# A graph layer on one core: the second pair's norm one call later, x + h on GpSimd, and the first matrix quarter loaded ahead of the second block of x

## The chip, the cores and the metric

One core of one Trainium2 chip. The metric is the device time of one launch in microseconds (us). The kernel before takes 1369.55 us, the median of three runs (1368.07 to 1371.08).

The core's engines are named as the profile names them: PE (TensorE, matrix products and transposes, results in PSUM), PEld (its weight load), DVE (VectorE), ACT (ScalarE), POOL (GpSimd) and SP (SyncE, which here only issues transfers). SPq and ACTq are the queues on which SP and ACT issue DMA transfers. Each engine works through its own instructions strictly in the order of the program and waits on semaphores for the others.

## The reference

A relational graph layer with a gate, over N = 1250 nodes of D = 1024 features and 20000 edges of 8 types, all in float32:

```python
h = relu(layernorm(x))
u = h @ root + bias
for r in range(8):
    mask = (edge_type == r)
    sums = segment_sum(h[src] * mask[:, None], dst, N)
    cnt = segment_sum(mask, dst, N)
    u = u + (sums / max(cnt, 1)[:, None]) @ weight[r]
z = concat([u, h], axis=1) @ w_gate + b_gate
out = x + tanh(u) * z + h * (1 - z)
```

The output can be written as (x + h) + z * (tanh(u) - h). The kernel stores x + h early, in the DRAM tensor `xh_dram`, and fetches it again in its last stage.

## The kernel before

**Matrix passes.** There are eleven matrices of 1024 x 1024: eight weights, root, and the two halves of w_gate. Pass s multiplies h by matrix s (s = 0 to 9); the last pass, with u, is written out separately. h is held in transposed form, five pairs of 128-row blocks: pair i is the blocks i and i + 5, in the buffer `h_op[i]`. A product of one pair with one matrix is `product()`: a Strassen form with seven products of quarters of 512 x 512 instead of eight. Seven operands come from each side: A11, A12, A21, A22 are the transposed quarters of h, and S1 to S4 are sums of them made by `left()` on DVE (L275). On the matrix side b11, b12, b21 and b22 are loaded quarters, and t1 to t4 are differences made by `make_t1()` to `make_t4()` on DVE (L167, L171, L175, L179). b12 is loaded into t3's buffer by `load_next()`.

After each quarter product PE goes on with the next; its PSUM bank is taken over by ACT (copies L330, L337, L341, L316, L359) or DVE (L309, L317, L325). PE accumulates in two banks, b and c, so it must wait for the copy out of b before it may add the next but one product into it: before S2 for L330, before S3 for L341.

**The order of the work.** The schedule is written by hand: whatever is called first stands first on its engine's queue. `product()` calls `between(j)` after each of its quarter products (j = 0 to 6). In pass 0, `between` takes one step of the generator `index()`, which runs two generators side by side: `norms()` (the layer norm, transposes and stores of the pairs 1 to 4) and `columns()` (the edge tables). A `yield` in `norms()` thus means "go on after the next quarter product". Pass 0, pair 0 has its own order: after A11 comes `second_block()`, which transposes the second block and makes the operands, then A12, S1, S2, S4, S3, A22.

**One pair's norm.** `both(a, b)` gives the order for the two blocks of a pair: statistics on DVE (L579, L583), the square root on ACT (L584), reciprocal and the negated scaled mean on DVE (L588, L589, both on 128 x 1), then h = relu(scale * x + less) on ACT (L605). `store()` writes h to `h_dram` from SP's queue; `factored()` transposes it on PE and evicts it, A11 or A21 on ACT (L266), A12 or A22 on DVE (L264). `with_x()` adds x + h on DVE (L615, 128 x 1024) and issues its store on SP's queue (L616). The sums of pair 2 write into h's own place or into the buffer of x; x of its first block lies in the S1 and S2 places of `h_op[2]`, so `left(h_op[2])` must come after that sum. The h of pairs 0, 2, 3 and one block of pair 4 share the scratch in `h_op[4]`. The buffers named `xt` are three, used in turn: a later load of x waits for the x + h store of the block that had the buffer.

**The start.** At the top, SP's queue carries the first half of each of the two x blocks of pair 0, then b11 (`load_first()`), b21, b12, b22, the x of pair 1 and of pair 2, then the edge lists. ACT's queue carries the second halves of the two x blocks. Block 0 is normed in halves on DVE (`centre(2)`, L598), transposed, and its relu is in the eviction (L262, L266); block 5 is normed with two relus on ACT (`relu(2)`), and `second_block()` transposes it. The relu of block 0's own h, L686, comes after that.

GpSimd makes the identity and a few fills at the start, the two iotas of `columns()`, and two fills of the last block's padding; from 124 us on it issues the scatters and gathers of the edges.

Of the kernel before, what the change touches and what calls it, by code (L numbers as in the profile page):

```python
# [19 lines left out]
def tile_rgcn_highway(  # L20
# [31 lines left out]
    nc = tc.nc  # L52
# [37 lines left out]
    def nrows(d):  # L90
        return min(P, N - d * P)
# [4 lines left out]
    def nedges(c):  # L96
        return P if c < NCH - 1 else EL
# [83 lines left out]
    class Second:  # L181
# [22 lines left out]
        def left(self):  # L204
            nc.vector.tensor_add(self.s1, self.a21, self.a22)
            nc.vector.tensor_sub(self.s2, self.s1, self.a11)
            nc.vector.tensor_sub(self.s3, self.a11, self.a21)
            nc.vector.tensor_sub(self.s4, self.a12, self.s2)
# [43 lines left out]
    def transposed(aop, part, of, n, relu=False):  # L252


        for half, to in enumerate(((A11, A12), (A21, A22))[part]):
            p = bank().rearrange("p (k f) -> p k f", k=KQ)
            for i in range(KQ):
                k = KQ * half + i
                nc.tensor.transpose(p[:, i, :n], of[:n, k * P:(k + 1) * P], ident[:n, :n])  # L259
            to_n, p_n = aop[:, to, :, :n], p[:, :, :n]  # L260
            if half and relu:
                nc.vector.tensor_scalar_max(to_n, p_n, 0.0)  # L262
            elif half:
                nc.vector.tensor_copy(to_n, p_n)  # L264
            else:
                nc.scalar.activation(to_n, p_n, AF.Relu if relu else AF.Copy)  # L266
            if n < P:
                nc.gpsimd.memset(aop[:, to, :, n:], 0.0)
# [103 lines left out]
    fac = []  # L372
# [173 lines left out]
    with ExitStack() as early:  # L546
# [6 lines left out]
        def load_x(i, part, t=None, pieces=1):  # L553
            d = i + part * NP
            n = nrows(d)
            if t is None:
                t = xpool.tile([P, D], F32, name="xt")
            for j in range(pieces):
                at = slice(j * D // pieces, (j + 1) * D // pieces)
                (nc.scalar if j else nc.sync).dma_start(t[:n, at], x[d * P:d * P + n, at])  # L560
            return t

        def scratch(i, part):

            return h_op[i][:, 2 * part:2 * part + 2].rearrange("p a k f -> p (a k f)")

        class Normed:
# [44 lines left out]
            def with_x(self, to=None):  # L612
                n = self.n
                to = self.xt if to is None else to
                nc.vector.tensor_add(to[:n], self.xt[:n], self.ht[:n])  # L615
                nc.sync.dma_start(xh_dram[self.d * P:self.d * P + n, :], to[:n])  # L616

        def both(a, b):

            a.stats(0)  # L620
            a.stats(1)
            a.spread()
            b.stats(0)
            a.scale()
            a.relu()
            b.stats(1)
            b.spread()
            b.scale()
            b.relu()

        def factored(i, blocks):
            for part in range(2):
                transposed(h_op[i], part, blocks[part].ht, blocks[part].n)


        warm = xpool.tile([P, 1], F32, name="warm")
        x0 = [load_x(0, part, pieces=2) for part in range(2)]
        nc.scalar.activation(warm, eps, AF.Sqrt)
        fac[0].load_first()
        fac[0].load_b21()  # L640
        fac[0].load_next()
        fac[0].load_b22()
# [21 lines left out]
        b0 = [Normed(part * NP, x0[part], scratch(NP - 1, part)) for part in range(2)]  # L664
# [285 lines left out]
                    yield  # L950

        def norms():
            yield
            yield
            both(*b1)
            fac[0].make_t4()
            for b in b1:
                b.store()
            yield
            yield  # L960
            yield
            factored(1, b1)
            left(h_op[1])
            yield
            for b in b0:
                b.with_x()
            x3 = [load_x(3, part) for part in range(2)]
            b2 = [Normed(2 + part * NP, x2[part], scratch(NP - 1, part)) for part in range(2)]
            both(*b2)
            yield  # L970
            for b in b2:
                b.store()
            yield
            for b in b1:
                b.with_x()
            yield
            factored(2, b2)
            b2[0].with_x(b2[0].ht)
            b2[1].with_x()
            left(h_op[2])  # L980
            x4 = [load_x(4, 0)]
            yield
            yield
            b3 = [Normed(3 + part * NP, x3[part], scratch(NP - 1, part)) for part in range(2)]
            both(*b3)
            yield
            for b in b3:
                b.store()
            yield
            factored(3, b3)  # L990
            left(h_op[3])
            yield
            for b in b3:
                b.with_x()
            x4.append(load_x(4, 1))
            yield
            for part in range(2):
                ht = xpool.tile([P, D], F32, name="xt") if part else scratch(NP - 1, 1)
                b = Normed(4 + part * NP, x4[part], ht)
                b.stats(0)  # L1000
                b.stats(1)
                b.spread()
                b.scale()
                b.relu()
                b.store()
                yield
                transposed(h_op[4], part, b.ht, b.n)
                b.with_x()
                yield
            left(h_op[4])  # L1010
            first_part.close()

        def index():
            for _ in zip_longest(norms(), columns()):
                yield
            with tc.tile_pool(name="ix", bufs=2) as ix:
                yield from slots(ix)
            yield from order()
# [17 lines left out]
    with ExitStack() as edges_part:  # L1036
# [167 lines left out]
        with tc.If(passes > 0):  # L1204
# [30 lines left out]
            with tc.For_i(0, passes, 1):  # L1235
# [9 lines left out]
                for c in range(NCH):  # L1245
                    n = nedges(c)
# [117 lines left out]
        for i in range(NP):  # L1364
# [55 lines left out]
            else:  # L1420
                product(h_op[i % 2], fac[NM - 1], t, between=beside_last, last=finish_last,
                        pieces=2, second=lambda: None,
# [24 lines left out]
```

## Time and profile before

The profile is of one execution, which took 1366.53 us by the clock of the runs; its span, from first to last instruction, is 1364.7 us.

| | |
|---|---|
| median of the runs | 1369.55 us |
| profiled execution | 1366.53 us |
| its span | 1364.7 us |
| PE busy | 1349.9 us, 99% |
| DVE busy | 932.9 us, 68% |
| POOL busy | 638.8 us, 47% |
| ACT busy | 365.7 us, 27% |
| PE busy in 0 to 104 us | 95.31 us |
| PE busy in 104 to 1364.7 us | 1254.59 of 1260.7 us |
| POOL busy in 0 to 104 us | 2.08 us |
| granted PE clock | full throughout |
| L615, one x + h on DVE | 1.22 us |
| L275, one sum of operands | 0.69 us |
| one quarter product on PE (eight instructions) | about 3.45 us |

The busy shares are averages over the whole kernel. What can change the time is where PE stands still, and that is read from the waits. A line of the timeline gives start, length, engine, line of the code, operation, output and inputs, shape, how many instructions it merges, and in brackets how long its engine had stood idle before it and what released it.

### The profile page before, as it was taken

What the parts mean: (1) busy time and instruction counts of PE and PEld (TensorE: products, weight loads), DVE (VectorE), ACT (ScalarE), POOL (GpSimd) and SP (SyncE); (2) the same over time, 40 slices, a digit from 0 to 9 for tenths busy, and PEclk for the clock granted to TensorE, in tenths of its full rate; (3) what the DMA queues carried; (4) which work ended last, traced back from release to release, by engine and by line L of the source; (5) the groups of instructions that cost most, each with busy time, mean ns of one, the idle gap of its engine ahead of it and who ended that gap; (6) DMA issues with size and microseconds to landing.
All of it is one profiled execution on the core that took longest, in us unless ns stands there. A gap on an engine that the chain in (4) does not pass through costs nothing.

```text
span 1364.7 us, 12816 instructions
## 1 busy us (share of the span) xinstructions
PE 1349.9 (99%) x3810; PEld 659.9 (48%) x3810; DVE 932.9 (68%) x1849; ACT 365.7 (27%) x792; POOL 638.8 (47%) x571
## 2 busy tenths in 40 slices
PE   8999999999999999999999999999999999999998
PEld 4444455455445544544554454455445445544443
DVE  6855887887885946567565756765664586567985
ACT  3235566566631111111111111111111111121220
POOL 0002655665561464557774435465443344435641
PEclk9999999999999999999999999999999999999999
DMA  8654565855663175379788627787965664586861
GB/s 312 253 196 131 121 139 134 191 115 114 158 167 93 61 206 137 116 250 254 218 282 315 213 81 287 264 303 258 347 217 201 217 239 149 194 284 219 294 205 58
DMA packets 110202, 272.77 MB, mean 200 GB/s; under 512 B 25956, under 2 KB 27986, under 8 KB 110000
## 3 DMA queue, kind: packets, MB, share of 16 engines
q0 software_dynamic: 48912, 128.60, 29.5%
q1 hardware_dynamic: 45088, 111.34, 26.3%
q10 hardware_dynamic: 16128, 31.98, 7.9%
q8 instruction: 30, 0.49, 0.2%
q14 instruction: 44, 0.36, 0.1%
HBM read 214.20 MB, written 80.65 MB: 216 GB/s over the span
## 4 chain that ended last, share of the span: by engine, by line
PE 91%; issue 4%; DVE 2%; POOL 1%; DMA 1%; ACT 0%; SPq 0%; POOLq 0%; DVEq 0%; ACTq 0%
PE ps L292 82%; PE ps L212 8%; PE ps L259 1%; PE ps_n L802 1%; DMA w<-in_L_gnn_weight_dram 1%; POOL out_dram L496 1%; DVE h_op L275 0%; PE ps_q L853 0%; POOL got L490 0%; DMA xt<-in_x_dram 0%; DVE st L579 0%; DMA xh_dram<-xt 0%; DVE h_op L615 0%; DVE w L171 0%; DVE h_op L264 0%
## 5 line engine op out<-in xcount | busy, mean ns | idle before, releaser
L292 PE MATMUL ps<-w,h_op 128*128 128x512 f32 x2800 | 1224.5, 593 | 6.2 <-ACT row L341 2.6
L292 PEld LDWEIGHTS ps<-w,h_op 128*128 128x128 f32 x2800 | 526.6, 190 | 620.2 <-issue 601.5
L1061 POOL DMA_INDIRECT got<-y,idx x202 | 256.0, 1267 | 265.7 <-DVE u L1069 197.2
L1069 DVE SCALAR_TENSOR_TENSOR u<-got,w_of,u 128x1024 f32<-128x1024 f32 (+1 forms) x192 | 246.0, 1283 | 127.6 <-DMA got<-y,idx 125.1
L881 POOL DMA_INDIRECT table<-row_col,at_i x157 | 180.2, 1148 | 154.1 <-DVE at_i L877 73.3
L317 DVE TENSOR_TENSOR row<-row,part 128x512 f32<-128x512 f32 x55 | 38.0, 690 | 109.6 <-ACT part L316 109.6
L359 ACT COPY row<-ps 128x512 f32<-128x512 f32 x50 | 29.3, 585 | 239.0 <-PE ps L292 234.1
L316 ACT COPY part<-ps 128x512 f32<-128x512 f32 x55 | 32.2, 585 | 179.8 <-PE ps L292 176.6
L309 DVE TENSOR_TENSOR row<-row,ps 128x512 f32<-128x512 f32 x54 | 36.9, 684 | 57.3 <-PE ps L292 53.3
L330 ACT COPY row<-ps 128x512 f32<-128x512 f32 x55 | 32.2, 586 | 163.2 <-PE ps L292 163.2
L337 ACT COPY row<-ps 128x512 f32<-128x512 f32 x55 | 32.2, 586 | 147.9 <-PE ps L292 144.3
L212 PE MATMUL ps<-w,w 128*128 128x256 f32 x288 | 71.3, 380 | 0.0
L341 ACT COPY row<-ps 128x512 f32<-128x512 f32 x55 | 32.2, 586 | 139.3 <-PE ps L292 139.3
L212 PEld LDWEIGHTS ps<-w,w 128*128 128x128 f32 x288 | 54.4, 190 | 20.9 <-issue 15.3
L807 DVE TENSOR_TENSOR seen<-seen,ps_n 128x110 f32<-128x110 f32 x157 | 42.1, 268 | 25.1 <-PE ps_n L802 20.8
L867 DVE SCALAR_TENSOR_TENSOR junk<-k_bc,key_col,before 128x128 f32<-128x128 int32 x157 | 54.9, 350 | 4.2
L527 POOL DMA_INDIRECT node_dram<-ids,pos_i x30 | 37.4, 1247 | 43.2 <-issue 42.9
L212 PE MATMUL ps<-w,h_op 128*128 128x256 f32 x216 | 56.0, 382 | 0.0
L935 DVE SCALAR_TENSOR_TENSOR junk<-v_bc,val,one 128x1280 bf16<-128x1280 f32 x30 | 46.6, 1554 | 9.5 <-DMA v_bc<-val_dram 8.7
L212 PEld LDWEIGHTS ps<-w,h_op 128*128 128x128 f32 x216 | 40.5, 190 | 25.3 <-issue 22.2
L784 ACT ACTIVATE is_lo<-io,less_lo 128x128 bf16<-128x128 f32 x157 | 50.1, 391 | 4.8 <-DMA xh_dram<-xt 4.8
L490 POOL DMA_INDIRECT u<-u_dram,node x20 | 22.9, 1145 | 51.3 <-DMA last_dram<-u 34.9
(187 smaller groups left out, 957.8 us busy)
## 6 DMA issues: line engine op xcount, KB each, us to landing
y<-row SPq DMA_DIRECT2D x72, 512.0 KB, 5.6
w<-in_L_gnn_weight_dram ACTq DMA_DIRECT2D x21, 1024.0 KB, 10.1
w<-in_L_gnn_weight_dram SPq DMA_DIRECT2D x11, 1024.0 KB, 13.3
k_bc<-keys_dram SPq DMA_DIRECT2D x39, 256.0 KB, 4.2
l_bc<-los_dram SPq DMA_DIRECT2D x39, 256.0 KB, 8.4
w<-in_L_gnn_w_gate_dram ACTq DMA_DIRECT2D x6, 1024.0 KB
h_dram<-h_op SPq DMA_DIRECT2D x9, 512.0 KB, 2.9
hr_dram<-row SPq DMA_DIRECT2D x9, 512.0 KB, 6.7
```

What stands on the lines that cost most here:

```text
L212: nc.tensor.matmul(p, a[:, k, :], b[:, k, :], start=(fresh and k == 0), stop=(k == 1), skip_group_check=True)
L292: nc.tensor.matmul(b[:, at], aop[:, i, k, :], w.of[i][:, k, at], start=(fresh and k == 0), stop=(k == KQ - 1), skip_group_check=True)
L309: nc.vector.tensor_add(c12, c12, c)
L317: nc.vector.tensor_add(c22, c22, d)
L527: ins = nc.gpsimd.indirect_dma_start(out=node_dram[g][:, :], out_offset=bass.IndirectOffsetOnAxis(ap=pos_i[:, g, d:d + 1], axis=0), in_=id ...
L784: nc.scalar.activation(is_lo[:, i, :], io, AF.Abs, bias=less_lo[:, c0 + i:c0 + i + 1])
L807: nc.vector.tensor_add(seen[j][:, i, :], was, p[:, i, :])
L867: nc.vector.scalar_tensor_tensor(junk, o["k_bc"][:, i, :], key_col[:, c:c + 1], before, op0=OP.is_equal, op1=OP.mult, accum_out=rank[:, c: ...
L881: ins = nc.gpsimd.indirect_dma_start(out=table[:, :], out_offset=bass.IndirectOffsetOnAxis(ap=at_i[:n, i:i + 1], axis=0), in_=row_col[:n, ...
L935: nc.vector.scalar_tensor_tensor(junk, v_bc[:, g, :], val[:, c:c + 1], one.to_broadcast([P, KEYS]), op0=OP.is_gt, op1=OP.mult, accum_out=p ...
L1061: nc.gpsimd.indirect_dma_start(out=t[:n], out_offset=None, in_=y[g][:, :], in_offset=bass.IndirectOffsetOnAxis(ap=at[:n, d, k:k + 1], axis=0),
L1069: nc.vector.scalar_tensor_tensor(u[:n], t[:n], w, u[:n], op0=OP.mult, op1=OP.add)
```

## The change

Three edits, all in pass 0. In `with_x()` the addition is issued on GpSimd instead of DVE; there are ten of them, for all ten blocks. At the top, b11's load stands between the loads of the two x blocks: on SP's queue the order becomes first half of block 0, b11, first half of block 5, b21, and so on; ACT's queue is unchanged. In `norms()` the norm of pair 1 is called one step later, after S2 and its copy instead of after S1, and the two sums of pair 0 move from the step in which pair 2's norm is called to the step after pair 1's norm.

```diff
             def with_x(self, to=None):
                 n = self.n
                 to = self.xt if to is None else to
-                nc.vector.tensor_add(to[:n], self.xt[:n], self.ht[:n])
+                nc.gpsimd.tensor_add(to[:n], self.xt[:n], self.ht[:n])
                 nc.sync.dma_start(xh_dram[self.d * P:self.d * P + n, :], to[:n])
...
         warm = xpool.tile([P, 1], F32, name="warm")
-        x0 = [load_x(0, part, pieces=2) for part in range(2)]
+        x0 = [load_x(0, 0, pieces=2)]
+        fac[0].load_first()
+        x0.append(load_x(0, 1, pieces=2))
         nc.scalar.activation(warm, eps, AF.Sqrt)
-        fac[0].load_first()
         fac[0].load_b21()
         fac[0].load_next()
         fac[0].load_b22()
...
         def norms():
-            yield
-            yield
+            for _ in range(3):
+                yield
             both(*b1)
             fac[0].make_t4()
             for b in b1:
                 b.store()
             yield
-            yield
+            for b in b0:
+                b.with_x()
             yield
             factored(1, b1)
             left(h_op[1])
             yield
-            for b in b0:
-                b.with_x()
             x3 = [load_x(3, part) for part in range(2)]
             b2 = [Normed(2 + part * NP, x2[part], scratch(NP - 1, part)) for part in range(2)]
             both(*b2)
```

On ACT the copy L341 now stands ahead of the two pairs of L584 and L605 of pair 1, instead of behind them. On DVE the order of everything but L615 is the same. On SP's queue a load of the next matrix (b12 of matrix 1) comes ahead of pair 1's two h stores. On POOL the sums of pairs 0, 1 and 2 come ahead of the two iotas, and those of pairs 3 and 4 around the padding fills.

## The prediction

> **What bounds the kernel now.** The page comes first: TensorE (PE) is busy 1349.9 of 1364.7 us at full clock, so a change can only matter where PE stands still. The table of waits for PE, over the first 104 us and over the rest, says where that is.
>
> ```profile
> PE ps L292 <- ACT row L341: 2.6, 1, 2.6
> PE ps L292 <- ACT row L330: 1.6, 1, 1.6
> PE ps L292 <- DMA w<-in_L_gnn_weight_dram: 1.3, 1, 1.3
> PE ps L259 <- ACT xt L605: 0.8, 1, 0.8
> PE ps L748 <- DVE h_op L264: 0.5, 1, 0.5
> ```
>
> Each line is who waits for whom, total us, count, longest. After 104 us the same table has one wait of 0.7 us, so all that can be won or lost lies in the first two matrix passes. The timeline of ScalarE (ACT) shows the largest wait: the copy that PE needs, L341, stands behind the second pair's norm.
>
> ```profile
> 26.46 1.24 ACT L605 ACTIVATE h_op<-h_op,less,rs 128x1024 f32<-128x1024 f32 x1 [0.52 <-DVE less L589]
> 27.61 0.28 ACT L584 ACTIVATE sd<-mv,eps 128x1 f32<-128x1 f32 x1
> 28.31 1.24 ACT L605 ACTIVATE h_op<-h_op,less,rs 128x1024 f32<-128x1024 f32 x1 [0.42 <-DVE less L589]
> 29.46 0.56 ACT L341 COPY row<-ps 128x512 f32<-128x512 f32 x1
> ```
>
> The timeline of VectorE (DVE) shows how little room the first product has (start, length, operation): operands without a gap from 14.35 to 23.5.
>
> ```profile
> 14.35 1.22 DVE L167 TENSOR_TENSOR w<-w,w 128x1024 f32<-128x1024 f32 x1
> 15.48 0.68 DVE L275 TENSOR_TENSOR h_op<-h_op 128x512 f32<-128x512 f32 x1
> 16.09 1.22 DVE L167 TENSOR_TENSOR w<-w,w 128x1024 f32<-128x1024 f32 x1
> 17.22 0.68 DVE L275 TENSOR_TENSOR h_op<-h_op 128x512 f32<-128x512 f32 x1
> 17.82 2.35 DVE L171 TENSOR_TENSOR w<-w,w 128x1024 f32<-128x1024 f32 x2
> 20.09 1.28 DVE L275 TENSOR_TENSOR h_op<-h_op 128x512 f32<-128x512 f32 x2
> 21.30 2.28 DVE L175 TENSOR_TENSOR w<-w,w 128x2048 f32<-128x2048 f32 x1
> ```
>
> PE runs four products from 13.54 to 27.44, 3.475 us each, so they begin at 13.54, 17.0, 20.5 and 23.97. The second needs the L275 that ends at 16.16 (0.85 us early), the third the first L171, ready at about 19.03 (1.47 us early).
>
> [...] A tiny POOL operation or a gather's reading of its indices, put beside two-input VectorE work, ends only after VectorE's next boundary:
>
> ```profile
> 475.12 0.67 POOL L540 TENSOR_SCALAR node_key<-node 128x10 int32<-128x10 int32 x1 [2.77 <-DMA node<-node_dram]
> 474.12 1.55 DVE L935 SCALAR_TENSOR_TENSOR junk<-v_bc,val,one 128x1280 bf16<-128x1280 f32 x1
> 560.65 0.25 POOL L540 TENSOR_SCALAR node_key<-node 128x10 int32<-128x10 int32 x1
> 708.14 1.92 POOL L1061 DMA_INDIRECT got<-y,idx  x1 [0.92 <-DVE u L1069]
> 706.58 3.93 DVE L1069 SCALAR_TENSOR_TENSOR u<-got,w_of,u 128x1024 f32<-128x1024 f32 x3 [0.53 <-DMA got<-y,idx]
> ```
>
> L540 takes 0.25 us with a PSUM operation beside it and 0.67 when L935 runs until 475.67. The gather takes 1.92 instead of its median 1.015: L1069's second piece ends near 709.2, 0.9 before the gather does. So POOL is let in at the first boundary of back-to-back VectorE work. That a long POOL operation holds VectorE likewise, no line here shows. [...]
>
> **The change part by part.** Times below are the profiled execution's (span 1364.7, reported as 1366.5; the median of the runs, 1369.55, is 3.0 higher, and I add the sum of shifts to the median).
>
> 1. Start. Before, the first quarter b11 lands about 9.03 (PE starts 9.16), behind 1 MB of x: 2.1 MB in some 7 us, 0.3 MB/us. Standing ahead of a 256 KB piece of x, it lands 0.85 earlier, 8.2, and the first product runs 8.3 to 11.8. But that piece now ends the same queue, at about 9.0, and VectorE reads it first. In the trace the second block's stats began at 7.03 and its two relu halves ended 10.56 and 11.28; 2.05 later they end 12.6 and 13.35. PE's last four transposes follow at 13.4, the next product at 13.9 instead of 13.54: +0.35. Bounds: landing at 7.85 or before gives -0.85, at 10 +1.3.
>
> 2. The norm one call later. The program order puts L341 ahead of the two L584/L605 pairs on ACT; VectorE's order there is unchanged. L341 then runs at once: -2.63. What is late next: the transposes of that pair's h, 3.5 us after; the relu ended at 29.55 and PE would come at 31, so covered if nothing slows VectorE. Its store also moves behind a weight load on SP's queue (from 29.95 to about 25), which nobody waits for.
>
> 3. The sums. Ten VectorE adds of 1.22 us go, ten POOL adds of 2.3 come, in POOL's own order, each as soon as its own inputs allow. POOL is idle between 2.3 and 124 us but for two memsets, so its own length is covered; what it holds up is VectorE.
> - First pair: ready when ACT's relu L686 ends, 14.9 before, about 15.4 now. That is inside the chain shown above. At the next two boundaries of VectorE POOL takes 2.3 us each, so L171 is 4.6 late against 1.47 of slack: +3.15 on PE. Bounds 0 (the sums don't hold VectorE, or wait until 23.5) and +5.
> - Second pair: the first sum starts as the first relu ends (27.70 before) and holds VectorE's L589, which has two SBUF inputs and stood at 28.12. The second relu is 1.9 late, ends 36.4; PE, at 34.5 by now, has 0.9 us of other transposes: +1.1. The second sum goes between L179 and L317; L317, L264, L275 and the next norm follow. Without POOL, dropping 2.35 us of L615 ahead of the stats at 41.36 would have removed the wait for L330 (47.33 against 45.82). With it the stats begin about 44.0 and L330 ends 5.97 later, 49.97, with PE there at 47.75: 2.25 instead of 1.57, so +0.7. Bounds -1.57 and +1.5.
> - Bank wait: L264 no longer stands behind the L615 at 51.06 and 52.20: -0.48.
> - Third pair: L275 waits for the first of its sums, which waits for the h store. Columns and SP's queue are 2.65 late, so the store lands about 57.7 (55.08 before). Sums to 60.0 and 62.3, back to back; L275 ends 65.0 instead of 60.06. POOL's iotas come behind the sums (62.5), still ahead of L764. The fourth pair's norm, next on VectorE, begins 68.6 instead of 63.62, and its own first sum holds L589 once more: relus end 72.2 and 76.0. PE would be at those transposes at 70.5: it waits 1.8 and then 2.75, +4.5. This is the least certain term: 0 to +6, as it leans on a landing and on two sums running together.
> - The rest (fourth and fifth pairs' sums) lies beside 14 us of matmuls; the wait of 0.85 for L605 at 88.3 is made by PE's own S4 product and stays.
>
> Sum: 0.35 - 2.63 + 3.15 + 1.1 + 0.7 - 0.48 + 4.5 = +6.7, rounded down to +6.5 as the last term can only shrink if a landing is early: 1373.0 for a profiled execution, 1376.0 against the median.
>
> **The rivals.**
> A. The two engines run side by side[...] (no trace shows the contrary direction). Then 0.35 - 2.63 - 1.57 - 0.48 = -4.3: 1365.2. For it: three waits are hit exactly, and VectorE's spacing beside gathers, 1.31 us per L1069, is hardly stretched; against it: those read few bytes. It decides if VectorE's L275 at 15.5 keeps its 0.68 us.
> B. POOL is held, but gets in mostly where VectorE has one input (stats, PSUM reads), or its add is nearer 1.3 us. Then the first term is about 0 to +1 and the fourth-pair term about +1.5: total near 0, 1369.5. For it: stats and evictions are a third of VectorE's work here; against it: the boundary of 708.
> C. Start alone: x's piece lands late, at 10, and the load edit costs 1.3 (or gains 0.85). It moves any case by less than 1.2, and is inside their ranges. That the reordering wins nothing, since the second block is then what PE waits for, is my forecast of that part.
>
> **How the numbers follow.** 0.2% is 2.7 us, about what a measurement here can tell from none. Held VectorE 0.60 (own range 1371 to 1380), A 0.30 (1363.5 to 1367), B 0.10. The range from 1364.5 to 1379.5 leaves out some of A and the top of the first. Held VectorE gives slower but for a small part: slower 0.58, faster 0.30, same 0.12.
>
> **What would show it.** Right: VectorE's L275 or L167 after 15.5 lasting 2 to 3.5 us, or gaps there ended by POOL; L341 at about 27 with no norm before it; new PE waits near 19, 22, 36 and 71; POOL adds of 2.3 us or more. Wrong: VectorE's durations unchanged beside POOL (A), sums much shorter than 2 us, or b11 and the second x block both early.

## The result and the profile after

The changed kernel takes 1377.24 us (median of six runs, 1376.28 to 1378.90) against 1369.07 for the kernel before in the same comparison (1367.71 to 1371.08). The ratio is 1.0061, 95% interval 1.0048 to 1.0074: slower by 8 us. Forecast were 1376.0 us and "slower".

The table of waits for PE of the changed kernel (who waits for whom, total us, count, longest):

```profile
PE ps L259 <- ACT h_op L605: 5.8, 4, 2.7
PE ps L292 <- issue: 2.6, 2, 1.8
PE ps L292 <- ACT row L330: 2.1, 1, 2.1
...
PE ps L292 <- DVE h_op L275: 1.3, 1, 1.3
PE ps L292 <- DVE w L167: 1.2, 1, 1.2
```

The wait of 2.6 for L341, which headed this table before, is gone: the norm edit did its work. In its place stand waits for operands, L275 and L167, and for relus, L605. The timeline of VectorE and of POOL (start, length, operation, number merged) shows what made the operands late:

```profile
14.58 1.22 DVE L167 TENSOR_TENSOR w<-w,w 128x1024 f32<-128x1024 f32 x1
15.71 2.83 DVE L275 TENSOR_TENSOR h_op<-h_op 128x512 f32<-128x512 f32 x1
18.47 3.36 DVE L167 TENSOR_TENSOR w<-w,w 128x1024 f32<-128x1024 f32 x1
...
32.65 2.02 DVE L589 SCALAR_TENSOR_TENSOR less<-mv,rs 128x1 f32<-128x1 f32 x1
...
59.95 4.87 DVE L275 TENSOR_TENSOR h_op<-h_op 128x512 f32<-128x512 f32 x4 [4.09 <-POOL h_op L615]
...
72.36 2.02 DVE L589 SCALAR_TENSOR_TENSOR less<-mv,rs 128x1 f32<-128x1 f32 x1
```

```profile
15.22 5.53 POOL L615 TENSOR_TENSOR xt<-xt,h_op 128x1024 f32<-128x1024 f32 x2 [13.23 <-ACT h_op L687]
...
36.03 3.06 POOL L615 TENSOR_TENSOR h_op<-h_op 128x1024 f32<-128x1024 f32 x1 [1.37 <-ACT h_op L605]
...
57.58 2.35 POOL L615 TENSOR_TENSOR h_op<-h_op,h_op 128x1024 f32<-128x1024 f32 x1 [18.49 <-DMA h_dram<-h_op]
```

Before, all of this on VectorE:

```profile
28.12 0.16 DVE L589 SCALAR_TENSOR_TENSOR less<-mv,rs 128x1 f32<-128x1 f32 x1
...
55.13 1.22 DVE L615 TENSOR_TENSOR h_op<-h_op,h_op 128x1024 f32<-128x1024 f32 x1 [0.51 <-DMA h_dram<-h_op]
56.27 1.22 DVE L615 TENSOR_TENSOR xt<-xt,h_op 128x1024 f32<-128x1024 f32 x1
57.40 2.74 DVE L275 TENSOR_TENSOR h_op<-h_op 128x512 f32<-128x512 f32 x4
```

L275 takes 2.83 us where it took 0.68, the next L167 3.36 where it took 1.22. Both were stretched by about 2.15 us, a little less than one POOL add (2.34 us where it runs alone). POOL's two sums, which run beside them, took 5.53 instead of 4.7. L589, an instruction of 128 x 1 that takes 0.16, is held for 1.9 us. In these lines the time spent held lies inside the record of the held instruction, not in a gap ahead of it: it is read from lengths, not from the column of idle time. Instructions that read PSUM keep their lengths beside a sum (L309 at 36.80 takes 0.68; L264 at 77.78 and 90.27, beside one for most of their length, 0.69 each).

For the third pair one can ask whether GpSimd's sum is merely late. L275 ends 4.68 us later than before (64.82 for 60.14). Of this 2.45 is the start of the first sum, which waits for the h store (57.58 for 55.13), and 2.13 is the hold (the first L275 takes 2.81). The slower add accounts for only 0.1: L275 starts 2.37 after that sum has begun, 2.27 before, as VectorE had both sums to do ahead of it.

The timeline of PE, at the place where the largest part was lost:

```profile
72.00 1.09 PE L259 MATMUL ps<-ident,h_op 128*128 128x128 f32 x8 [1.80 <-ACT h_op L605]
75.77 1.97 PE L259 MATMUL ps<-ident,h_op 128*128 128x128 f32 x8 [2.67 <-ACT h_op L605]
77.53 11.77 PE L292 MATMUL ps<-w,h_op 128*128 128x512 f32 x24
```

and the same 24 matmuls before:

```profile
70.11 10.47 PE L292 MATMUL ps<-w,h_op 128*128 128x512 f32 x24
```

The two waits for relus, 1.80 and 2.67, are what the prediction had: the first follows from the late L275 at 59.95, the second from the L589 held at 72.36. (The trace puts the second relu's release down to POOL's sum, which ends when L589 does, near 74.4. In e11 the two lie apart: PE's transposes behind that relu start at 70.89, so the relu, of 1.24 us, started at about 69.6, while POOL's copies run from 68.38 to 70.52.) What it didn't have is the length of the lines themselves: eight transposes at 1.97 instead of 1.09, and 24 matmuls at 11.77 instead of 10.47. The table by stretches of time gives the reason (stretch, its length, PE busy, number of instructions, granted clock, share of the DMA engines, GB/s):

```profile
70.00:72.00 2.00, 0.21 (x1) 1.00 0.00 0
...
74.00:76.00 2.00, 0.23 (x1) 0.50 0.01 4
...
78.00:80.00 2.00, 2.00 (x3) 0.50 1.01 403
...
82.00:84.00 2.00, 2.00 (x7) 1.00 0.46 184
```

The granted clock is at half, 0.50, from about 73.3 to 80.2 us. Together the two lines are 2.2 us longer.

### The profile page after: what moved, and what is told of

The parts are those of the page before. It is cut to its first block, busy times and chain, and to the rows that moved or that the text cites. A ratio compares the mean times of both kernels' runs of the same rounds, so it can differ in the third digit from the quotient of the medians.

```text
span 1375.6 us, 12823 instructions
## 1 busy us (share of the span) xinstructions
PE 1353.6 (98%) x3810; PEld 660.6 (48%) x3810; DVE 934.2 (68%) x1839; ACT 365.4 (27%) x792; POOL 659.8 (48%) x581
## 4 chain that ended last, share of the span: by engine, by line
PE 83%; issue 6%; DVE 3%; POOL 2%; DMA 1%; ACT 0%; SPq 0%; POOLq 0%; DVEq 0%
PE ps L292 74%; PE ps L212 8%; POOL got L490 1%; PE ps_n L803 1%; DMA got<-hr_dram,node 1%; POOL out_dram L496 1%; DVE row L1373 0%; DMA got<-y,idx 0%; DVE h_op L1319 0%; POOL xt L615 0%; PE ps_q L854 0%; DMA h_dram<-h_op 0%; DVE h_op L275 0%; DVE row L1374 0%; DVE u L1272 0%
## 5 line engine op out<-in xcount | busy, mean ns | idle before, releaser
L317 DVE TENSOR_TENSOR row<-row,part 128x512 f32<-128x512 f32 x55 | 41.2, 750 | 107.8 <-ACT part L316 107.3
L316 ACT COPY part<-ps 128x512 f32<-128x512 f32 x55 | 32.1, 584 | 174.0 <-PE ps L292 160.6
L330 ACT COPY row<-ps 128x512 f32<-128x512 f32 x55 | 32.1, 584 | 163.8 <-PE ps L292 158.5
L309 DVE TENSOR_TENSOR row<-row,ps 128x512 f32<-128x512 f32 x54 | 36.9, 683 | 56.2 <-PE ps L292 52.7
L341 ACT COPY row<-ps 128x512 f32<-128x512 f32 x55 | 32.2, 585 | 143.5 <-PE ps L292 138.1
L167 DVE TENSOR_TENSOR w<-w,w 128x2048 f32<-128x2048 f32 (+1 forms) x12 | 27.5, 2291 | 26.7 <-PE ps L292 22.3
```

Source lines behind the costliest of these rows:

```text
L309: nc.vector.tensor_add(c12, c12, c)
L317: nc.vector.tensor_add(c22, c22, d)
```

## The experiments

The theory, "holding": while a GpSimd add that reads SBUF runs, VectorE's instructions with two SBUF inputs stand still, and the sums lie where such instructions feed PE. The rivals: the norm's or the load's new place made the loss; or GpSimd is merely slower, so that its results come late; or any GpSimd work holds VectorE. Each ratio is to the kernel before on the same chip. Chips differ by some 3 us (the kernel before took 1367.6 to 1370.4 on them), so the ratio is what counts; "about" times below are ratio times 1369.07. Beside it stands the start of PE's first matmul for the edge slots, the end of the norms' stage in the trace: 103.66 us before, 112.39 in the changed kernel.

| kernel | ratio (95%) | end of the stage |
|---|---|---|
| changed kernel | 1.0061 (1.0048 to 1.0074) | 112.39 |
| e1, all sums on VectorE | 0.9975 (0.9967 to 0.9982) | 100.61 |
| e2, sums on GpSimd alone | 1.0082 (1.0066 to 1.0098) | 116.83 |
| e3, no load edit | 1.0059 (1.0043 to 1.0075) | 111.72 |
| e4, fills instead of sums | 0.9958 (0.9943 to 0.9973) | 98.52 |
| e5, pair 0 on VectorE | 1.0031 (1.0020 to 1.0042) | 108.36 |
| e6, pairs 2 and 3 on VectorE | 1.0015 (1.0008 to 1.0022) | 105.99 |
| e7, pair 0 gated, pair 1 moved | 0.9993 (0.9985 to 1.0001) | 101.30 |
| e8, second norm later, pair 1 moved | 0.9995 (0.9987 to 1.0003) | 104.64 |
| e9, pair 0 gated | 0.9972 (0.9964 to 0.9981) | 99.74 |
| e10, pair 0 gated, pair 1 still later | 1.0024 (1.0015 to 1.0032) | 106.03 |
| e11, copies instead of sums | 1.0015 (1.0007 to 1.0024) | 105.37 |
| e12, norm edit alone | 0.9973 (0.9966 to 0.9979) | 100.92 |

**Which of the three edits costs the time: e1, e2, e3, e12.** One edit undone (e1, e3) or made alone (e2, e12).

e1 against the changed kernel:

```diff
-                nc.gpsimd.tensor_add(to[:n], self.xt[:n], self.ht[:n])
+                nc.vector.tensor_add(to[:n], self.xt[:n], self.ht[:n])
```

e3 against the changed kernel:

```diff
-        x0 = [load_x(0, 0, pieces=2)]
-        fac[0].load_first()
-        x0.append(load_x(0, 1, pieces=2))
+        x0 = [load_x(0, part, pieces=2) for part in range(2)]
         nc.scalar.activation(warm, eps, AF.Sqrt)
+        fac[0].load_first()
```

e2 is the kernel before with the first of these edits the other way round; e12 has both of them.

> The changed kernel with its ten x + h sums issued on VectorE again; the load order, the norm one call later and the new place of pair 0's two sums are kept. Holding theory (GpSimd's long adds hold VectorE's instructions with two SBUF inputs): the L341 wait of 2.6 us stays away, pair 0's sums fall into VectorE's idle stretch of 3.4 us ahead of L317, so that the next norm starts 2.3 us sooner and the wait of 1.6 for L330 goes too; the start gives back 0.2. About -4: 1364 to 1366.5, no wait for L275 or L167, L275 at 0.68 us each, and no granted clock below 0.95 near 75 us. Rival (the norm's or the load's new place made the loss, the sums' engine is incidental): 1373 to 1378, with the waits near 72 and 76 us still there.

> The kernel before with one edit, the sums on GpSimd; norm and loads in their old places. Holding theory: the whole loss of the first and third pairs (2.5 near 19 to 22 us, 6 to 7 near 70 to 80), and on top L341 behind a norm whose L589 is held: wait 4 to 5 instead of 2.6. 1377 to 1383. Rival (norm or load made the loss): 1367 to 1371.

> The changed kernel with b11's load behind both first halves of x again. My step 1 (the early quarter only moves the wait to the second x block, 0.2 to 0.35 lost): within 0.6 of the changed kernel, 1376.5 to 1377.5, A11 on PE at 9.2 us again and the second product at about 13.5. Rival (the load order made the loss): 1369 to 1372. Rival (the load edit gains): 1378 or more.

> The kernel before with one edit, pair 1's norm one call later and pair 0's two sums (on VectorE) in their new place; loads in the old order. The wait of 2.6 for L341 goes and 0.6 of the 1.6 for L330, so -3.2 and what the load order is worth here: within 0.7 of the kernel that has the load edit too (0.9975 of before). Rival (the load edit carried that gain): 1368 or more against 1369.

With all sums on VectorE (e1) the kernel is 3.4 us faster than before; with the sums on GpSimd as the only edit (e2) it is 11 us slower. The engine of the sums thus costs 11 to 12 us, in either surrounding, and the norm edit is worth about 3. In e2 the wait for L341 grew to 5.64, where 4 to 5 was expected, with a clock of 0.50 from 34.1 to 40.9 us. The load order is worth nothing that can be measured: 1.0059 against 1.0061 with GpSimd's sums (e3), 0.9973 against 0.9975 without (e12). One item of e1's expectation failed: of the 1.6 us of waiting for L330, 1.0 stayed. The 3.4 us of VectorE's idle time ahead of L317 were there only because PE waited for L341; with that wait gone L316 was done at 31.9, and L317, at 33.66 behind the two sums, was late after all.

**Reading, writing or mere lateness: e4 and e11.** Both leave the sum x + h out of the output and put other GpSimd work in its place, of about the same length. A fill needs no input, so it can stand earlier than the sum, and L275 of the third pair needn't wait for it (it starts at 49.10); e4 thus takes away that wait along with the holding.

e4 against the changed kernel:

```diff
-                nc.gpsimd.tensor_add(to[:n], self.xt[:n], self.ht[:n])
+                for _ in range(2):
+                    nc.gpsimd.memset(to[:n], 0.0)
```

e11 against the changed kernel:

```diff
-                nc.gpsimd.tensor_add(to[:n], self.xt[:n], self.ht[:n])
+                for _ in range(2):
+                    nc.gpsimd.tensor_copy(to[:n], (self.ht if to is self.xt else self.xt)[:n])
```

> The changed kernel with each x + h on GpSimd replaced by two fills of the sum's place with zeros (128 x 1024, 0.98 us each by the fill of line 1054, so about 2 us where the add took 2.35), so GpSimd writes SBUF for nearly as long but reads nothing; x + h is left out of the output. If GpSimd's reads hold VectorE: L275 and L167 after 15.5 keep 0.68 and 1.22 us, no PE wait for either, L589 0.16 us, and what stays is GpSimd's own length behind the h store near 58 us (third pair's L275 up to 2 us late, little of it on PE): 1364 to 1368. If any GpSimd work of that length holds VectorE, or only its lateness counts: 1374 to 1377, with L275 at 2 us or more.

> The changed kernel with each x + h on GpSimd replaced by two copies of h (or of x) into the sum's place, so GpSimd reads one input instead of two for about as long; x + h is left out of the output. If reading SBUF is what holds VectorE: L275 and L167 after 15.5 are stretched by about one copy's length each, L589 as well, and the time is 1371 to 1378. If it takes GpSimd's two inputs: L275 0.68, L167 1.22, L589 0.16 us and 1363 to 1368, as with the fills.

The fills (e4), POOL and then VectorE:

```profile
13.22 1.96 POOL L616 MEMSET xt<- 128x1024 f32 x2 [4.15 <-ACT h_op L605]
27.93 3.86 POOL L616 MEMSET h_op<- 128x1024 f32 x4 [12.74 <-ACT h_op L605]
```

```profile
14.52 1.22 DVE L167 TENSOR_TENSOR w<-w,w 128x1024 f32<-128x1024 f32 x1
...
28.29 0.16 DVE L589 SCALAR_TENSOR_TENSOR less<-mv,rs 128x1 f32<-128x1 f32 x1
28.36 2.28 DVE L179 TENSOR_TENSOR w<-w,w 128x2048 f32<-128x2048 f32 x1
```

A fill runs until 15.18 beside L167, and four run from 27.93 to 31.79 across L589 and L179: all three keep their lengths of before, 1.22, 0.16 and 2.28. At 84.48 a fill stands beside L317, which reads two inputs from SBUF: it takes 0.69, where it takes 2.48 beside a sum in the changed kernel. Time 0.9958, about 1363.3, a little below the range expected. This is about what the kernel would gain if the sums cost nothing.

The fills aren't harmless to everything, though. At one place they run beside VectorE instructions with one SBUF input (`columns()`), POOL and then VectorE:

```profile
52.12 1.96 POOL L616 MEMSET h_op<- 128x1024 f32 x2 [20.33 <-DMA h_dram<-h_op]
54.02 2.06 POOL L616 MEMSET xt<- 128x1024 f32 x2
```

```profile
53.69 0.49 DVE L755 CAST kcol_i<-key_col 128x157 int32<-128x157 f32 x1
54.21 0.95 DVE L757 TENSOR_SCALAR part_i<-kcol_i 128x157 int32<-128x157 int32 x1
55.19 0.97 DVE L758 TENSOR_SCALAR less_lo<-part_i 128x157 f32<-128x157 int32 x1
56.20 0.24 DVE L759 TENSOR_SCALAR part_i<-kcol_i 128x157 int32<-128x157 int32 x1
```

L755, L757 and L758 take 0.24 each in e10 (58.18 to 58.97), where no GpSimd sum runs beside them; here they take 0.49, 0.95 and 0.97, and as soon as the fills are over L759 is back at 0.24. So having one input didn't keep these VectorE instructions at their length. No run puts such a cast or scalar operation beside a GpSimd add.

The copies (e11):

```profile
15.76 1.52 DVE L275 TENSOR_TENSOR h_op<-h_op 128x512 f32<-128x512 f32 x1
17.20 2.05 DVE L167 TENSOR_TENSOR w<-w,w 128x1024 f32<-128x1024 f32 x1
19.18 1.52 DVE L275 TENSOR_TENSOR h_op<-h_op 128x512 f32<-128x512 f32 x1
```

```profile
15.24 6.36 POOL L616 COPY xt<-h_op 128x1024 f32<-128x1024 f32 x4 [13.25 <-ACT h_op L688]
...
68.38 2.14 POOL L616 COPY xt<-h_op 128x1024 f32<-128x1024 f32 x2 [8.77 <-ACT h_op L605]
```

Each VectorE instruction is 0.83 us longer, a little less than one copy (2.14 for two where they run alone), and the three shown, with the L171 behind them, are stretched one after the other while POOL does its four copies in 6.36 instead of 4.28. These lengths fit a handing over in turn: after each POOL instruction one of VectorE's is let in, and after each of VectorE's one of POOL's. Time 1.0015, about 1371.1. So what held VectorE's instructions with two SBUF inputs here was neither the number of GpSimd's inputs nor its writing: the adds and the copies, which read SBUF, lengthened L275 by 2.15 and 0.83 us, and the fills, which only write, left L167, L589 and L179 at their 1.22, 0.16 and 2.28.

**Where the loss sits, and the slow clock: e5 and e6.** Sums of some pairs go back to VectorE; e5 against the changed kernel (e6 has `(2, 3)` for `(0,)`):

```diff
-                nc.gpsimd.tensor_add(to[:n], self.xt[:n], self.ht[:n])
+                eng = nc.vector if self.d % NP in (0,) else nc.gpsimd
+                eng.tensor_add(to[:n], self.xt[:n], self.ht[:n])
```

> The changed kernel with only pair 0's two x + h sums on VectorE, the other eight on GpSimd. Holding theory: PE's waits for L275 and L167 near 19 and 22 us (1.3 + 1.2) go; pair 1's adds still hold L589 and L179, and the two sums (2.35) now stand ahead of L317, so the wait for L330 (2.1) may grow by up to 1.5; the loss near 72 to 80 us stays with its slow clock. 1373.5 to 1376.5. Rival (the first collision is not what costs): 1377 or more, with the waits near 19 and 22 still there.

> The changed kernel with the four sums of pairs 2 and 3 on VectorE, the other six on GpSimd. Holding theory, with the slow clock as a result of the two waits: the waits of 1.8 and 2.7 for L605 go, and with them the granted clock of 0.50 near 74 to 80 us; about 6.7 less than the changed kernel, 1369.5 to 1371.5, with the waits near 19, 22 and 48 us still there. Rival (only the waits go, the slow clock has another cause): 1372 to 1373.5 with a clock below 0.9 somewhere in 66 to 90 us.

In e6 the waits near 72 us are 0.35 in all, and the clock stays full (1.00 in every 2 us from 66 to 84); PE's lines there are as before:

```profile
71.52 1.09 PE L259 MATMUL ps<-ident,h_op 128*128 128x128 f32 x8 [0.35 <-ACT h_op L605]
72.45 10.46 PE L292 MATMUL ps<-w,h_op 128*128 128x512 f32 x24
```

The stage ends 6.4 us sooner than in the changed kernel, and the time is about 1371.1: 6.1 less than the changed kernel where 6.7 was expected for waits and slow clock together. With the waits the fall of the clock is gone too, so the rival, a slow clock with another cause, falls. In e5 the waits near 19 and 22 us are gone, but the stage ends 4.0 us sooner, about 1373.3, just below the range expected, and with other parts:

```profile
47.65 6.74 PE L292 MATMUL ps<-w,h_op 128*128 128x512 f32 x8 [4.25 <-ACT row L330]
...
73.88 1.09 PE L259 MATMUL ps<-ident,h_op 128*128 128x128 f32 x8 [1.81 <-ACT h_op L605]
```

The wait for L330 doubles, as the two VectorE sums are themselves held by pair 1's add (3.91 instead of 2.35), and this pause of 4.25 brings its own slow clock, 0.50 from 47.0 to 53.8 us: eight matmuls take 6.74 instead of 3.70. In return the pair near 72 us, for which PE now comes later, costs one wait of 1.81 and no slow clock (its transposes keep 1.09). The terms of such a sum are not independent: what is lost early is in part paid back by a later wait.

**The same adds at another time: e9.** Pair 0's sums are on GpSimd again, but behind a flag that VectorE sets when it begins the statistics of pair 1, which have one SBUF input; all other sums are on VectorE. Against e1, with `flag` a tile of 128 x 1 and `with_x()` taking the engine as an argument, VectorE where none is given:

```diff
             for _ in range(3):
                 yield
+            nc.vector.memset(flag, 0.0)
+            nc.gpsimd.memset(flag, 1.0)
             both(*b1)
...
             for b in b0:
-                b.with_x()
+                b.with_x(eng=nc.gpsimd)
```

> As the gated kernel, with pair 1's two sums back ahead of L264 where the other kernels have them; so it is the kernel with all sums on VectorE plus one difference, pair 0's sums on GpSimd beside pair 1's statistics. Holding theory: no wait for L330, the bank wait of 0.5 is back, the waits of 1.5 and 0.8 for L605 near 65 us are gone or below 0.7 in all: PE reaches its fourth transposes at about 64 us and the time is 1363.5 to 1365.5. Rival (the waits at 65 us come from pair 0's sums on GpSimd and not from pair 1's moved ones): they stay, 1365.5 to 1367.5.

```profile
24.82 4.68 POOL L615 TENSOR_TENSOR xt<-xt,h_op 128x1024 f32<-128x1024 f32 x2
```

```profile
25.14 0.68 DVE L579 BATCH_NORM_STATS2 st<-h_op 128x6 f32<-128x512 f32 x1
...
26.72 0.47 DVE L589 SCALAR_TENSOR_TENSOR less<-mv,rs 128x1 f32<-128x1 f32 x1
...
28.88 0.63 DVE L589 SCALAR_TENSOR_TENSOR less<-mv,rs 128x1 f32<-128x1 f32 x1
```

The adds take 4.68, 2.34 each, so nothing holds POOL here. The statistics keep 0.68; L589 is held by 0.3 and 0.5, until the sum beside it ends, and PE doesn't wait for it. No wait for L275, L167 or L330 is left. The stage ends 0.9 us before that of e1, but the time, 0.9972, can't be told from e1's or e12's. That the place decides and not the operation alone is shown by the lengths; that gating is worth having over plain VectorE sums isn't shown.

**Three that missed: e7, e8, e10.** They tried to win the bank wait of 0.5 (e1) as well, by moving pair 1's two VectorE sums from their place ahead of pair 2's L264: in e7 and e8 behind pair 2's L275, in e10 behind pair 3's norm. e8 has no sum on GpSimd and has pair 2's norm one call later instead.

e7 against e9:

```diff
-            for b in b1:
-                b.with_x()
             yield
             factored(2, b2)
             b2[0].with_x(b2[0].ht)
             b2[1].with_x()
             left(h_op[2])
+            for b in b1:
+                b.with_x()
```

e8 has the same move against e1, and `both(*b2)` behind the `yield` that followed it. e10 against e9:

```diff
-            for b in b1:
-                b.with_x()
             yield
             factored(2, b2)
...
             both(*b3)
+            for b in b1:
+                b.with_x()
```

> The load and norm edits kept; pair 0's two sums on GpSimd but held back by a one-element-per-row flag until VectorE has done L325 and begins the statistics of pair 1 (one SBUF input); all other sums on VectorE, pair 1's two behind pair 2's L275. Holding theory (it is when the adds stand, not that they are on GpSimd): the first sum lies beside statistics, L589 and L179 are held by less than 1.5 us in all, none of it on PE; L317 is free early, so the wait for L330 (1.0 with all sums on VectorE) and the bank wait (0.5) go: 1363.5 to 1366, no L275 or L167 wait near 19 to 22 us. Rival (a long GpSimd add slows VectorE's one-input work too): statistics (L579) at over 0.9 us each and 1368 or more.

> No sums on GpSimd: as with all sums on VectorE, and pair 2's norm one call later too (L330 ahead of its two relus on ScalarE), pair 1's sums behind pair 2's L275. Expected: the waits for L330 (1.0) and for the bank (0.5) go, 1364.5 to 1366 against 1366.8. Rival (the relus, now behind L330, come late for the transposes near 47 us): a wait for L605 of 1 us or more there and no gain, 1366.5 to 1368.

> As the gated kernel, with pair 1's two sums behind pair 3's norm instead of behind pair 2's L275. Expected: neither the bank wait nor the waits for L605 near 65 us, 1363 to 1365. Rival (the sums, now ahead of L325, hold up a bank or L264 and give 1 to 2 us back): 1365 to 1367, with a wait for L325 or L264.

In e7 and e8 PE is ahead of e1 by 2 us at 49.5 us, as meant, and then waits for the fourth pair's relus, 1.5 + 0.8 and 3.1 + 0.8; in e8 the clock falls too, to 0.50 from 68.5 to 71.9 us. That pair 0's GpSimd sums aren't to blame is what e9 shows, where these waits are 0.34. The timeline of VectorE shows it: in e9 pair 1's sums are done at 49.0, while VectorE would otherwise wait for an h store, which ends its idle time at 51.20; in e7 they run at 55.44, behind that wait, and the fourth pair's statistics begin at 61.26 instead of 59.69. Time that looked lost to the bank wait was time that the store covered. This explains the lost gain, not all of the time: in the traces e7 ends the stage only 0.7 us behind e1, while its ratio is about 2.5 us above e1's. The execution traced of e7 (1364.14) was its fastest of 13, and what the others lose isn't shown. e10 is slower than before, for another reason:

```profile
68.61 0.69 DVE L264 COPY h_op<-ps 128x512 f32<-128x512 f32 x1 [1.11 <-DMA xh_dram<-h_op]
71.38 0.69 DVE L264 COPY h_op<-ps 128x512 f32<-128x512 f32 x1 [2.07 <-DMA xh_dram<-h_op]
```

Pair 1's sums are written to `h_op[3]`, the buffer into which pair 3's transposes are evicted, so L264 and L266 wait for the stores of the sums to land. On VectorE L275 and the statistics of the fifth pair's first block come that much later, its relu with them, and PE pauses 3.6 us for it, with a clock of 0.50 from 81.9 to 85.3 us behind the pause. At about 1372.4 it is above both ranges expected.

## Why the prediction held, and where its sum was off

The steps, with the shift of PE's start against before where PE's lines can be paired:

- **Start**: forecast +0.35. The second product starts at 13.78 instead of 13.54, +0.24. Right, and worth nothing in the time (e3, e12).
- **Norm later**: forecast -2.63. L341 runs at 27.43 with no norm ahead of it (29.46 before, behind the norm), and nothing waits for it. Right; e12 shows its worth alone, with the sums at their new place on VectorE: 0.9973.
- **First pair's sums hold VectorE**: forecast +3.15; measured 1.32 + 1.24 = 2.56 in waits. The holding, the two instructions held (2.83 and 3.36 us) and the handing over at each boundary (two sums in 5.53) are as forecast. No line of before shows the 2.3 us reckoned for one sum on GpSimd; measured was 2.34. The sum had PE wait for L171, an operand of the product S2; PE waited one product earlier, in S1, for L275 and for the second L167, and no wait for L171 followed. With the steps above PE stands at +0.48 when it comes to the second pair's transposes (34.09 for 33.61), forecast +0.87. By these starts the step cost 2.87 (0.48 - 0.24 + 2.63), some 0.3 more than the two waits.
- **Second pair**: forecast +1.1, a wait for L330 of 2.25 and -0.48 for the bank; measured 0.88, 2.13 and no bank wait. The third pair's product starts at 56.21 for 54.50, +1.71, forecast +2.19.
- **Third and fourth pair**: forecast waits 1.8 and 2.75; measured 1.80 and 2.67. Here the sum lacked a term: the 2.2 us of slow clock that the two waits bring on. The first transposes of the fifth pair start at 89.14 for 80.41, +8.73, where the sum had +6.7. The earlier terms were some 0.5 too large, which hid part of it. The missing term has no fixed size: in e3, with waits of 1.90 and 2.68 at the same place, the clock is at half only from 75.9 to 79.3, 3.4 us with PE busy, and that costs 1.7.

From 89 us to the end both kernels run at the same distance, but for one PE pause of 1.84 at 196.19, put down to "issue". It is also in e2, e3, e10 and e11 (1.8 to 1.9, each 83.8 us after the end of the stage) and shorter or absent in the rest, the kernel before among these; what makes it isn't settled. With it the profiled executions differ by 10.85 us, while the medians differ by 8.2, where +6.5 was forecast: before's profiled execution was 2.5 us below its median. That the forecast of 1376.0 lies 1.2 us from the time measured is thus in part luck: it started from a median 0.5 above the one measured beside the changed kernel.

The holding theory was given 0.60 and is shown, by e1 and e2 for the cost and by e4, e9 and e11, with the lengths in the traces, for the holding itself. What in the chip makes the two engines wait for each other isn't shown. Rival A (side by side, -4.3) falls with the 2.83 us of L275, and e4 shows about what it would have given: 0.9958. Rival B (POOL gets in beside one-input work) doesn't hold for this kernel's order, but it is what e9 brings about by a flag. Rival C was right in that the load edit wins nothing.

## What to carry to other kernels

Moving an elementwise sum from VectorE to GpSimd freed VectorE here only where VectorE meanwhile had statistics (0.68 us beside a sum in e9) or work with PSUM (L309, 0.68); beside work with two SBUF inputs the GpSimd adds and copies held the VectorE instruction behind them until they ended (L275 2.83 and 1.52 us instead of 0.68), even one of 128 x 1 (L589, 2.02 instead of 0.16). Casts and scalar operations from SBUF to SBUF, with one input, are to be checked first: fills alone held them in e4 (up to 0.97 us instead of 0.24). So look at what stands on VectorE at the moment when the sum's inputs are ready, not at GpSimd's idle share, and where the sum must go there, hold it back until the statistics or the PSUM work. And when PE is made to wait, price the pause together with the clock that it may lose (2.2 us here behind waits of 1.80 and 2.67), and check whose buffer a moved instruction writes to.

## What the runs showed that had not been expected

The sum priced PE's pauses and no fall of the clock. Half clock (0.50) lasted 6.8 us in the changed kernel (73.3 to 80.2), in e5 (47.0 to 53.8) and in e2 (34.1 to 40.9 and 78.5 to 85.3), and 3.4 us in e3 (75.9 to 79.3), e8 (68.5 to 71.9) and e10 (81.9 to 85.3). In the changed kernel no single long pause went ahead of it: in the 3.1 us from the start of the first wait (70.2) to the fall, PE was busy with eight transposes for 1.09 us. Single pauses of 2.63 (before) and 2.13 (the changed kernel's wait for L330) cost no clock, nor did 1.07 + 1.43 (e11) or 1.49 + 0.81 (e7); 3.1 + 0.8 (e8), 3.6 (e10), 4.25 (e5), 5.64 (e2), 1.4 + 2.7 (e2) and 1.8 + 2.7 did. What length of pause, or how much work between two, decides it isn't shown.
